# Turning normalized tokens on VectorE in three more groups of a two-layer block, and bias loads on other DMA queues

## The chip, the cores and the metric

The kernel runs on one core of one Trainium2 chip. The metric is device time in microseconds (us), a median of several executions. The engines are TensorE (PE in the profile; PEld is its weight load), VectorE (DVE), ScalarE (ACT), GpSimd (POOL) and SyncE (SP). Each works through its own instructions in the order in which the program issued them, and they wait for one another by semaphores.

## The reference

Two layers work on an image batch of 2 x 56 x 56 positions with 384 channels, 6272 tokens in all, in float32.

Layer 0 is neighbourhood attention (12 heads of 32 channels, a 7 x 7 window that is shifted inwards at the border, a relative position bias) and a two-layer perceptron:

```
h = attention(layer_norm(x));  x = x + h @ w_proj + b_proj
y = layer_norm(x);             x = x + gelu(y @ w1 + b1) @ w2 + b2        # hidden 1536
```

Layer 1 projects to 768 channels, applies a depthwise 3 x 3 convolution, runs an exponential average along rows and columns in both directions, and ends with another perceptron:

```
p = layer_norm(x) @ w_in + b_in
local = depthwise_conv3x3(p)
mixed = 0.25 * (left_right + right_left + top_bottom + bottom_top)(local) + local
x = x + layer_norm(mixed) @ w_out + b_out
x = x + gelu(layer_norm(x) @ w1 + b1) @ w2 + b2
```

## The kernel before

**Three stages.** From 0 to about 700 us the attention of layer 0 runs in windows of 8 x 14 queries. There are 14 groups (two images, seven bands of 8 rows), four windows to a group, three steps to a window (one for each set of four heads), so 12 steps k in group n. Then comes the *first pass* (from about 700 to 1700 us, function `passes`, lines 1418 to 1490): it computes the perceptron of layer 0 and the input projection of layer 1 in 13 groups g of up to four tiles of 128 tokens (sizes 2, 3, 4, 4, ...). The *last pass* (lines 1512 to 1555) computes the output projection of layer 1 and its perceptron, in 13 groups with the sizes reversed.

**Beside the passes** VectorE works on the convolution and the averages. The class `Beside` holds a list of jobs, each a generator of steps. `beside.go(worth)`, called after each piece of matrix work, adds 0.9 (later 1.0) times `worth` to an account and issues steps until their estimated costs have used it up. This settles the order of VectorE's instructions when the program is built. Jobs are added at the end of `project_in` when enough rows of the image are there: the first at the end of group 3 of the first pass. `beside.busy()` says whether jobs are left. The last of them are finished before group 6 of the last pass takes its input (`half_way` is 6).

**Turning tokens into channels.** A layer norm works on tokens (a token on each partition), and the next matrix product needs channels on partitions. There are two ways:

- `channels` calls `to_channels` (line 251): TensorE multiplies each 128 x 128 block with the identity into PSUM (tag `pt`, three banks), 12 such turnings for four tiles of 384 channels, and ScalarE takes the result to SBUF with the norm's gain and shift (line 254).
- `turned` (line 1074) turns one tile on VectorE, SBUF to SBUF, in 16 instructions that each turn three 32 x 32 blocks. `scaled` (line 1081) then applies gain and shift on ScalarE, in place, in three instructions, one for each chunk of 128 channels.

In the first pass `by_vector` chooses: it is true where no convolution is under way, that is in groups 1, 2 and 3. In the last pass it is true from group 6 on.

**The order within a group of the first pass.** Twelve hidden columns (m = 0 to 11) each take three matmuls into one of three banks (`hidden`, line 1090) and one Gelu on ScalarE (line 1099). In their midst stands work on the group before (`waiting`: its tokens have gone through the perceptron of layer 0) and on the next group:

- m=1: `norm_w.shift` on VectorE (line 233), for the group before; m=2 to 5: its tiles are normalized by ScalarE (line 240);
- m=3 to 6, with `by_vector`: `turned` of these tiles on VectorE, one a column, issued ahead of the column;
- m=3: statistics of the next group's tiles on VectorE (line 214); m=5: their shift (line 233); m=7 to 10: ScalarE normalizes them;
- m=6: the group before is stored, after an addition of a row to it (line 1026, on VectorE while there are jobs);
- m=11: `scaled` or `channels` of the group before, ahead of the last column.

Then `project_in` (six columns with `w_in`, line 1090) reads that turned tile `hT_w`; then the next group's tokens are turned for the next hidden columns, and the second matrix of the perceptron is applied tile by tile (`tokens`, line 1106, 24 matmuls a tile, two banks in turn); VectorE adds the residual (line 1478) and takes statistics.

**The order within a group of the last pass.** Twelve hidden columns with the statistics of the next group beside them; `project_out` of the next group (line 1343 takes it); then `tokens` for k = 0 to 3 of this group, with the next group's turning in their midst: at k=1 and k=2 two tiles each on VectorE and `scaled` at k=3, or `channels` at k=3.

**The bias loads.** Attention adds a bias tile for each of three column places, in one buffer each, loaded anew when the band place or image changes: 18 loads, of 1344 KB or 2016 KB (line 317). The first three are issued on SP, the others on ACT's queue. The input x of a group (672 KB, line 302), the values of a window (line 466) and all stores (line 643) go by SP.

Of the kernel before, what the change touches and what calls it, by code (L numbers as in the profile page):

```python
# [40 lines left out]
B, H, W, C = 2, 56, 56, 384  # L41
NH, KS, HD = 12, 7, 32
P = 128
NC = C // P
INNER, NI = 2 * C, 2 * C // P
HID, NHID = 4 * C, 4 * C // P
# [10 lines left out]
NWC = W // QC  # L57
# [29 lines left out]
def place(i, n):  # L87

    return 0 if i == 0 else 2 if i == n - 1 else 1
# [84 lines left out]
def block_kernel(ctx: ExitStack, tc: tile.TileContext, ins: dict, out: bass.AP):  # L174
    nc = tc.nc
# [128 lines left out]
    def spans(place, n, e):  # L304
        return n if place == 1 else e

    def load_bias(n, j):

        b, g = groups_a[n]
        pr, pc = place(g, NG), place(j, NWC)  # L310
        if (b, pr, pc) in biases:
            return
        _, at, size = BIAS_T_AT[pr, pc]
        most = NH * TT * (3 if pc == 1 else 2)
        t = kp.tile([P, most], F32, name=f"bias{pc}")
        queue = nc.sync if n == 0 else nc.scalar
        queue.dma_start(out=t[:, :size], in_=ins["bias_t"][:, at : at + size])
        biases[b, pr, pc] = t[:, :size].rearrange("p (n c q) -> p n c q", n=NH, q=TT)

# [4 lines left out]
    for i in (1, 2, 0):  # L324
        nc.sync.dma_start(out=wqkv[:, :, i * C : (i + 1) * C], in_=w_src[:, :, i * C : (i + 1) * C])
    load_x(1)
    load_bias(0, 0)
    load_bias(0, 1)
    wproj = lp.tile([P, NC, C], F32, name="wproj")
    nc.sync.dma_start(out=wproj, in_=ins["L0_conv_w_proj"].rearrange("(c p) n -> p c n", p=P))  # L330
    shift = lp.tile([P, C], F32, name="shift")
    b_proj = ins["rows"][ROWS["b_proj"] : ROWS["b_proj"] + 1, :]
    nc.sync.dma_start(out=shift, in_=b_proj.to_broadcast([P, C]))
    bq = lp.tile([P, NC], F32, name="bq")


# [268 lines left out]
    groups, dgroups = grouped(sizes), grouped(sizes[::-1])  # L605
# [60 lines left out]
        measure_x(1, k)  # L666
    for m in range(NC, 2 * NC):
        query_or_key(0, m, any_bank)()
    for k in range(NT):
        normalize_x(1, k)  # L670
    for t in tiles_of(0):
# [39 lines left out]
    END, THEN = ng - 2, (7, 9, 11, 13, 16, 19, 22)  # L711
    for s in range(NU + 4):
        n, k, hg, i = s // UG, s % UG, s % NC, s // NC
# [30 lines left out]
        if k == 2 and n + 4 < ng:  # L744
            load_x(n + 4)
        if k == 1 and n < ng:
            load_bias(n, NWC - 1)
        if n + 1 < ng and k in (4, 10):
            load_bias(n + 1, 0 if k == 4 else 1)
        if s == NU - UG - 4:  # L750
            ectx.close()
            wm = ctx.enter_context(tc.tile_pool(name="w_mlp", bufs=1, side="right"))
# [23 lines left out]
        new, before, last = units.get(s), units.get(s - 1), units.pop(s - 2, None)  # L776
# [204 lines left out]
    def passes(xs, xn, w1, w2, between=lambda ps: None):  # L981
# [10 lines left out]
        last = len(groups) - 1  # L992
        half_way = next(g for g, (t, n) in enumerate(dgroups) if t + n * P > T1)
# [417 lines left out]
        for g, (t0, n) in enumerate(groups):  # L1411
            hid = []

            by_vector = 0 < g < last and not beside.busy()
            preparing = prepare_w_out() if g == 1 else iter(())
            if g == last:
                beside.until((0, NI - 1))
                load_row(0, "b2_1")
                ahead = load_mix(0)
            for m in range(NHID):  # L1420
                next(preparing, None)
                if waiting is not None:
                    gw, x2w, norm_w = waiting
                    if m == 1:
                        norm_w.shift(groups[gw][1])
                    if m == 2:
                        xn_w = xp.tile([P, NT, C], F32, name="xn")
                    if 2 <= m < 2 + groups[gw][1]:
                        norm_w.apply_by_scalar(m - 2, x2w, xn_w)
                    if by_vector and m == 2:  # L1430
                        hT_w = io.tile([P, NC, MT], F32, name="hT")
                    if by_vector and 3 <= m < 3 + groups[gw][1]:
                        turned(xn_w, m - 3, hT_w)
                    if m == (11 if g == 1 else 6):
                        store_x2(gw, x2w)
                    if m == NHID - 1 and by_vector:
                        scaled(hT_w, groups[gw][1], *n1)
                    elif m == NHID - 1:
                        hT_w = channels(xn_w, groups[gw][1], *n1)
                hid.append(hidden(w1, m, hT, n, "L0_conv_b1"))  # L1440
                if g < last:
                    if m == 3:
                        x_next, n_next = xs.pop(g + 1), groups[g + 1][1]
                        norm_next = norm_of(x_next, n_next, sm)
                        norm_next.close(n_next)
                    if m == 5:
                        norm_next.shift(n_next)
                    if m == 7:
                        xn_next = xp.tile([P, NT, C], F32, name="xn")
                    if 7 <= m < 7 + n_next:  # L1450
                        norm_next.apply_by_scalar(m - 7, x_next, xn_next)
                    if m == NHID - 1:
                        add_row(x_next, n_next, "b2_0")
                if g == last:
                    measure_beside(m, 0, ahead)
                beside.go(MLP)
            for _ in preparing:
                pass
            if g == 0:
                between(bank())  # L1460
            if waiting is not None:
                project_in(gw, hT_w)
            if g == last:
                w1, w2_1, w_parts = weights(1)
                for part in w_parts[:3]:
                    part()
            if by_vector:
                hT = io.tile([P, NC, MT], F32, name="hT")
                for k in range(n_next):
                    turned(xn_next, k, hT)  # L1470
                scaled(hT, n_next, *ln2)
            elif g < last:
                hT = channels(xn_next, n_next, *ln2)
            x2 = io.tile([P, NT, C], F32, name="xc")
            norm = Norm(sm)
            for k in range(n):
                ps = tokens(hid, w2, k)
                nc.vector.tensor_tensor(x2[:, k, :], ps, x[:, k, :], ALU.add)
                norm.add(k, [x2[:, k, :]])
                if g < last or k < n - 1:  # L1480
                    beside.go(ROW)
            norm.close(n)
            waiting = g, x2, norm
            if g + 2 <= last:
                xs[g + 2] = load_group(x1f, groups[g + 2], "xa")
            if g < last:
                x = x_next
# [4 lines left out]
        g, x2, norm_w = waiting  # L1492
# [17 lines left out]
        n2 = "L1_conv_n2_g", "L1_conv_n2_b"  # L1510
        hT = channels(first["xn"], dgroups[0][1], *n2)
        for g, (t0, n) in enumerate(dgroups):
            by_vector = half_way <= g < last
            hid = []
            for m in range(NHID):
                hid.append(hidden(w1, m, hT, n, "L1_conv_b1"))
                if g < last:
                    measure_beside(m, g + 1, ahead)
                beside.go(MLP_D)
            res = x3  # L1520
            if g < last:
                x3, norm = project_out(g + 1, *ahead)
            if g + 2 <= last and g + 2 != half_way:
                ahead = load_mix(g + 2)
            for k in range(n):
                if by_vector and 0 < k < n - 1:
                    for q in range(2 * k - 2, min(2 * k, dgroups[g + 1][1])):
                        turned(xn, q, hT)
                elif by_vector and k == n - 1:
                    scaled(hT, dgroups[g + 1][1], *n2)  # L1530
                elif k == n - 1 and g < last:
                    hT = channels(xn, dgroups[g + 1][1], *n2)
                ps = tokens(hid, w2, k)
                o = res[:, k, :]
                if k == 0 and g < last:
                    norm.shift(dgroups[g + 1][1])
                if k == 0 and by_vector:
                    xn = normalized(norm, x3, dgroups[g + 1][1])
                    hT = io.tile([P, NC, MT], F32, name="hT")
                if g == last and k == n - 1:  # L1540

                    assert ps is y_end and t0 + n * P == T2
                    nc.vector.tensor_copy(rows[:, 1, :], o)
                    break
                nc.vector.tensor_tensor(o, ps, o, ALU.add)
                nc.sync.dma_start(out=yout[t0 + k * P : t0 + (k + 1) * P, :], in_=o)
                if k == n - 3 and g < last:
                    if not by_vector:
                        xn = normalized(norm, x3, dgroups[g + 1][1])
                    add_row(x3, dgroups[g + 1][1], "b2_1")  # L1550
                beside.go(ROW_D)
            if g + 2 == half_way:
                ahead = load_mix(g + 2)
# [92 lines left out]
```

## Time and profile before

| what | us |
|---|---|
| median of 3 runs | 2662.26 (2661.57 to 2664.49) |
| the profiled execution's own time | 2662.15 |
| its span, first to last instruction | 2660.4 |
| TensorE busy | 2636.8 |
| VectorE busy | 1963.3 |
| ScalarE busy | 898.8 |
| GpSimd busy | 250.2 |
| VectorE, turning tokens (line 1074), 672 instructions of 269 ns | 181.0 |
| TensorE, turning tokens (line 251), 315 of them | 39.0 |
| VectorE, convolution taps (line 1184), 336 instructions | 377.1 |

A line of the timeline gives the start, the length, the engine, the line of the program, the operation, what it writes and reads, its shape and how many instructions are drawn together; in square brackets stands how long the engine was idle before it and what released it. Matmuls overlap each other, so the time between two starts is the price of what lies between them, and not the sum of the lengths. A line of the busy times by stage gives the stretch, its length, the busy time of each engine with its instructions, the granted clock of TensorE (1.00 is full speed), the share of the DMA engines that was busy, and GB/s.

### The profile page before, as it was taken

What the parts mean: (1) busy time and instruction counts of PE and PEld (TensorE: products, weight loads), DVE (VectorE), ACT (ScalarE), POOL (GpSimd) and SP (SyncE); (2) the same over time, 40 slices, a digit from 0 to 9 for tenths busy, and PEclk for the clock granted to TensorE, in tenths of its full rate; (3) what the DMA queues carried; (4) which work ended last, traced back from release to release, by engine and by line L of the source; (5) the groups of instructions that cost most, each with busy time, mean ns of one, the idle gap of its engine ahead of it and who ended that gap; (6) DMA issues with size and microseconds to landing.
All of it is one profiled execution on the core that took longest, in us unless ns stands there. A gap on an engine that the chain in (4) does not pass through costs nothing. (4 is left out here: it accounts for less than half of the span.)

```text
span 2660.4 us, 37315 instructions
## 1 busy us (share of the span) xinstructions
PE 2636.8 (99%) x14987; PEld 1472.0 (55%) x14987; DVE 1963.3 (74%) x3539; ACT 898.8 (34%) x1447; POOL 250.2 (9%) x264
## 2 busy tenths in 40 slices
PE   8999999999999999999999999999999999999999
PEld 5666656666655455555555555555555555555556
DVE  3878877876465698688998889889988737677652
ACT  4655555554322332223344422312134211111111
POOL 0111111110211100000010000000000011100100
PEclk9999999999999999999999999999999999999999
DMA  6422354224410132233346544433355410111000
GB/s 197 155 90 92 130 191 161 73 84 157 161 43 32 65 110 87 86 132 106 121 152 241 185 139 156 178 126 109 103 207 194 180 42 24 45 45 39 30 13 17
DMA packets 131927, 298.98 MB, mean 112 GB/s; under 512 B 10678, under 2 KB 87584, under 8 KB 129440
## 3 DMA queue, kind: packets, MB, share of 16 engines
q1 hardware_dynamic: 126800, 269.76, 29.4%
q10 hardware_dynamic: 4944, 26.74, 2.9%
q8 instruction: 119, 1.95, 0.3%
q14 instruction: 64, 0.52, 0.1%
HBM read 180.86 MB, written 115.61 MB: 111 GB/s over the span
## 5 line engine op out<-in xcount | busy, mean ns | idle before, releaser
L1090 PE MATMUL mm<-hT,w 128*128 128x512 f32 (+2 forms) x1872 | 769.4, 568 | 0.4 <-ACT hT L254 0.2
L1090 PEld LDWEIGHTS mm<-hT,w 128*128 128x128 f32 x1872 | 352.0, 190 | 383.0 <-issue 351.4
L1099 ACT ACTIVATE hid<-mm,chan 128x512 f32<-128x512 f32 (+2 forms) x312 | 206.1, 661 | 671.6 <-PE mm L1090 671.6
L1106 PE MATMUL y_end<-w,hid 128*128 128x384 f32 x1200 | 395.2, 486 | 0.0
L1184 DVE SCALAR_TENSOR_TENSOR loc<-pt,taps,loc 128x990 f32<-128x990 f32 (+9 forms) x336 | 377.1, 1122 | 10.0 <-ACT loc L1166 1.7
L1106 PE MATMUL y<-w,hid 128*128 128x384 f32 x1152 | 379.4, 486 | 0.0
L1106 PEld LDWEIGHTS y_end<-w,hid 128*128 128x128 f32 x1200 | 227.5, 190 | 157.2
L1106 PEld LDWEIGHTS y<-w,hid 128*128 128x128 f32 x1152 | 218.2, 190 | 150.5 <-issue 1.0
L531 DVE TENSOR_TENSOR pts<-sc,bias 119x448 f32<-119x448 f32 (+3 forms) x336 | 221.0, 700 | 72.1 <-PE sc L516 70.0
L537 ACT ACTIVATE pts<-pts 119x448 f32<-119x448 f32 (+3 forms) x336 | 206.6, 642 | 183.3 <-DVE pts L531 183.2
L222 POOL TENSOR_TENSOR rs<-rs,mhalf 128x4 f32<-128x4 f32 (+4 forms) x67 | 87.1, 1300 | 1729.0 <-DVE rs L219 1693.4
L387 PE MATMUL ps<-hT,wqkv 128*128 128x448 f32 x504 | 213.1, 561 | 5.3 <-ACT vs L432 3.2
L1074 DVE STREAM_TRANSPOSE hT<-xn 32x96 f32<-32x96 f32 x672 | 181.0, 269 | 31.3 <-PE mm L1090 11.7
L1090 PE MATMUL mm<-hT,w_in 128*128 128x512 f32 (+2 forms) x468 | 191.9, 568 | 0.6 <-ACT hT L254 0.6
L240 ACT ACTIVATE xn<-xc,sh,rs 128x384 f32<-128x384 f32 x98 | 64.7, 698 | 269.3 <-DVE sh L233 269.2
L1090 PEld LDWEIGHTS mm<-hT,w_in 128*128 128x128 f32 x468 | 88.5, 190 | 102.1 <-issue 90.6
L387 PEld LDWEIGHTS ps<-hT,wqkv 128*128 128x128 f32 x504 | 90.6, 192 | 86.8 <-issue 73.2
L516 PEld LDWEIGHTS sc<-qT,kT 32*100 32x100 f32 (+3 forms) x3168 | 90.7, 169 | 66.4 <-issue 16.0
L1316 DVE STREAM_TRANSPOSE turned<-mx 32x192 f32<-32x192 f32 x336 | 123.3, 367 | 4.2
L516 PE MATMUL sc<-qT,kT 32*100 32x112 f32 (+3 forms) x3168 | 113.4, 270 | 5.9 <-DVE pts L531 4.7
L557 PE MATMUL o<-pts,vt 100*32 100x112 f32 (+3 forms) x3168 | 111.2, 264 | 1.5 <-ACT og L479 1.0
L425 PE MATMUL ps<-wqkv,hT 128*128 128x384 f32 x294 | 106.9, 502 | 0.0
(106 smaller groups left out, 2645.1 us busy)
## 6 DMA issues: line engine op xcount, KB each, us to landing
loc<-loc_d SPq DMA_DIRECT2D x24, 784.0 KB
mixed<-mix_d SPq DMA_DIRECT2D x24, 784.0 KB
mix_d<-mixed SPq DMA_DIRECT2D x24, 784.0 KB
bias<-in_bias_t ACTq DMA_DIRECT2D x13, 1344.0 KB
xa<-x_d SPq DMA_DIRECT2D x22, 768.0 KB
p_d<-mx SPq DMA_DIRECT2D x10, 1536.0 KB
mx<-mix_d SPq DMA_DIRECT2D x10, 1536.0 KB
pt<-p_d SPq DMA_DIRECT2D x18, 560.0 KB
```

The lines of the kernel that those rows point to most:

```text
L387: nc.tensor.matmul(ps, lhsT=wqkv[:, c, m * P : (m + 1) * P], rhs=hT[:, c, half_of(n)], start=c == 0, stop=c == NC - 1,)
L425: nc.tensor.matmul(ps, lhsT=hT[:, c, at : at + P], rhs=wqkv[:, c, 2 * C :], start=c == 0, stop=c == NC - 1,)
L516: nc.tensor.matmul(sc[i // 2][: w.keys, i % 2, (first + c) * TT : (first + c + 1) * TT], lhsT=kT[d, hg, w.keys_at + r * w.kc : w.keys_at + ...
L531: nc.vector.tensor_tensor(self.of(half), sc[half][:n, :, at].rearrange("p h (c q) -> p h c q", q=TT), self.w.bias[:n, 4 * self.hg + h : 4 ...
L537: nc.scalar.activation(self.of(half), self.of(half), AF.Exp)
L557: nc.tensor.matmul(o[i * HD : (i + 1) * HD, hg, :], lhsT=w.vt[:n, c, h * HD : (h + 1) * HD], rhs=self.pts[:n, i, c, :], start=c == 0, stop ...
L1074: nc.vector.transpose(hT[j : j + HD, :, k * P + i : k * P + i + HD], xn[i : i + HD, k, :].rearrange("p (c q) -> p c q", c=NC)[:, :, j : j ...
L1090: nc.tensor.matmul(ps[:, : n * P], lhsT=w[:, c, m * P : (m + 1) * P], rhs=hT[:, c, : n * P], start=c == 0, stop=c == NC - 1,)
L1099: nc.scalar.activation(t[:, : n * P], ps[:, : n * P], AF.Gelu, bias=col(b1, m))
L1106: nc.tensor.matmul(ps, lhsT=t[:, k * P : (k + 1) * P], rhs=w[:, m, :], start=m == 0, stop=m == len(lhs) - 1,)
L1184: nc.vector.scalar_tensor_tensor(to, pt[:, lo + dy - self.top : hi + dy - self.top, xt : xt + n], self.tap(dy, dx), to, ALU.mult, ALU.add,)
L1316: nc.vector.transpose(t[j : j + HD].rearrange("p (m c) -> p m c", m=NI)[:, :, i : i + HD], mx[i : i + HD, :, k * P + j : k * P + j + HD],)
```

## The change

The first-pass groups 4 and 5, which have convolution beside them, turn the tokens of the group before by VectorE (`n1_by_vector`) in place of TensorE; the next group's tokens are still turned by TensorE there. The last pass turns by VectorE one group sooner: in group 5 for the tokens of group 6. The first two bias loads, the attention's output weights and a row are issued on ACT's queue after the first group's keys were computed, in place of SP's queue at the very start. The later bias loads are issued on SP, but for those of the last attention group, which stay on ACT.

```diff
--- before.py
+++ after.py
@@ -304,7 +304,7 @@
     def spans(place, n, e):
         return n if place == 1 else e
 
-    def load_bias(n, j):
+    def load_bias(n, j, queue=nc.sync):
 
         b, g = groups_a[n]
         pr, pc = place(g, NG), place(j, NWC)
@@ -313,7 +313,6 @@
         _, at, size = BIAS_T_AT[pr, pc]
         most = NH * TT * (3 if pc == 1 else 2)
         t = kp.tile([P, most], F32, name=f"bias{pc}")
-        queue = nc.sync if n == 0 else nc.scalar
         queue.dma_start(out=t[:, :size], in_=ins["bias_t"][:, at : at + size])
         biases[b, pr, pc] = t[:, :size].rearrange("p (n c q) -> p n c q", n=NH, q=TT)
 
@@ -324,13 +323,9 @@
     for i in (1, 2, 0):
         nc.sync.dma_start(out=wqkv[:, :, i * C : (i + 1) * C], in_=w_src[:, :, i * C : (i + 1) * C])
     load_x(1)
-    load_bias(0, 0)
-    load_bias(0, 1)
     wproj = lp.tile([P, NC, C], F32, name="wproj")
-    nc.sync.dma_start(out=wproj, in_=ins["L0_conv_w_proj"].rearrange("(c p) n -> p c n", p=P))
     shift = lp.tile([P, C], F32, name="shift")
     b_proj = ins["rows"][ROWS["b_proj"] : ROWS["b_proj"] + 1, :]
-    nc.sync.dma_start(out=shift, in_=b_proj.to_broadcast([P, C]))
     bq = lp.tile([P, NC], F32, name="bq")
 
 
@@ -666,6 +661,11 @@
         measure_x(1, k)
     for m in range(NC, 2 * NC):
         query_or_key(0, m, any_bank)()
+
+    load_bias(0, 0, nc.scalar)
+    nc.scalar.dma_start(out=wproj, in_=ins["L0_conv_w_proj"].rearrange("(c p) n -> p c n", p=P))
+    nc.scalar.dma_start(out=shift, in_=b_proj.to_broadcast([P, C]))
+    load_bias(0, 1, nc.scalar)
     for k in range(NT):
         normalize_x(1, k)
     for t in tiles_of(0):
@@ -744,9 +744,9 @@
         if k == 2 and n + 4 < ng:
             load_x(n + 4)
         if k == 1 and n < ng:
-            load_bias(n, NWC - 1)
+            load_bias(n, NWC - 1, nc.scalar if n > END else nc.sync)
         if n + 1 < ng and k in (4, 10):
-            load_bias(n + 1, 0 if k == 4 else 1)
+            load_bias(n + 1, 0 if k == 4 else 1, nc.scalar if n >= END else nc.sync)
         if s == NU - UG - 4:
             ectx.close()
             wm = ctx.enter_context(tc.tile_pool(name="w_mlp", bufs=1, side="right"))
@@ -1412,6 +1412,7 @@
             hid = []
 
             by_vector = 0 < g < last and not beside.busy()
+            n1_by_vector = by_vector or g in (4, 5)
             preparing = prepare_w_out() if g == 1 else iter(())
             if g == last:
                 beside.until((0, NI - 1))
@@ -1427,13 +1428,13 @@
                         xn_w = xp.tile([P, NT, C], F32, name="xn")
                     if 2 <= m < 2 + groups[gw][1]:
                         norm_w.apply_by_scalar(m - 2, x2w, xn_w)
-                    if by_vector and m == 2:
+                    if n1_by_vector and m == 2:
                         hT_w = io.tile([P, NC, MT], F32, name="hT")
-                    if by_vector and 3 <= m < 3 + groups[gw][1]:
+                    if n1_by_vector and 3 <= m < 3 + groups[gw][1]:
                         turned(xn_w, m - 3, hT_w)
                     if m == (11 if g == 1 else 6):
                         store_x2(gw, x2w)
-                    if m == NHID - 1 and by_vector:
+                    if m == NHID - 1 and n1_by_vector:
                         scaled(hT_w, groups[gw][1], *n1)
                     elif m == NHID - 1:
                         hT_w = channels(xn_w, groups[gw][1], *n1)
@@ -1510,7 +1511,7 @@
         n2 = "L1_conv_n2_g", "L1_conv_n2_b"
         hT = channels(first["xn"], dgroups[0][1], *n2)
         for g, (t0, n) in enumerate(dgroups):
-            by_vector = half_way <= g < last
+            by_vector = half_way - 1 <= g < last
             hid = []
             for m in range(NHID):
                 hid.append(hidden(w1, m, hT, n, "L1_conv_b1"))
```

## The prediction

> **What bounds the kernel now.** I read the page first, then the busy time by stage, then the timelines of TensorE, VectorE and ScalarE in the groups that the change touches.
>
> ```profile
> span 2660.4 us, 37315 instructions
> PE 2636.8 (99%) x14987; PEld 1472.0 (55%) x14987; DVE 1963.3 (74%) x3539; ACT 898.8 (34%) x1447; POOL 250.2 (9%) x264
> ```
>
> TensorE is busy for 99% of the span; its idle time is 2660.4 - 2636.8 = 23.6 us in all. So the end is set by TensorE's work plus its stalls, and a change can gain only what it takes off TensorE or out of these 23.6 us, but can lose much by a new wait in front of TensorE. By stage (columns: TensorE, weight loads, VectorE, ScalarE, GpSimd busy, clock, DMA share, GB/s):
>
> ```profile
> 868.00:945.00 77.00, 77.00 (x204) 38.57 (x203) 52.39 (x160) 22.53 (x33) 8.88 (x4) 1.00 0.16 56
> 945.00:1025.00 80.00, 80.00 (x230) 41.33 (x229) 67.81 (x68) 25.32 (x36) 3.92 (x2) 1.00 0.34 123
> 1025.00:1105.00 80.00, 80.00 (x230) 41.35 (x229) 52.60 (x57) 23.02 (x34) 4.95 (x2) 1.00 0.23 81
> ...
> 2107.00:2189.00 82.00, 82.00 (x255) 45.12 (x254) 25.32 (x42) 12.87 (x19) 12.28 (x5) 1.00 0.25 87
> ```
>
> These are first-pass groups 3, 4 and 5 and last-pass group 5. Over a whole group, VectorE seems to have room: 12.2 us in group 4, 27.4 us in group 5, 56.7 us in the last. What counts is where the room lies. TensorE in group 4:
>
> ```profile
> 945.02 28.49 PE L1090 MATMUL mm<-hT,w 128*128 128x512 f32 x66
> 973.34 1.47 PE L251 MATMUL tp<-ident,xn 128*128 128x128 f32 x12
> 974.65 2.74 PE L1090 MATMUL mm<-hT,w 128*128 128x512 f32 x6
> 977.23 15.61 PE L1090 MATMUL mm<-hT,w_in 128*128 128x512 f32 x36
> ```
>
> Eleven of twelve hidden columns, the 12 turnings that go, the last column, and at 977.23 the input projection, which reads what was turned. VectorE in the same group:
>
> ```profile
> 957.66 0.55 DVE L214 BATCH_NORM_STATS2 st<-xa 128x6 f32<-128x384 f32 x1
> ...
> 960.53 5.35 DVE L1184 SCALAR_TENSOR_TENSOR loc<-pt,taps,loc 128x1045 f32<-128x1045 f32 x4
> 965.79 0.15 DVE L233 SCALAR_TENSOR_TENSOR sh<-mv,rs 128x4 f32<-128x4 f32 x1
> ...
> 967.14 1.75 DVE L1026 TENSOR_TENSOR xc<-xc,rows 128x1536 f32<-128x1536 f32 x1
> ```
>
> 957.66 is the statistics of column m=3, 965.79 the shift of m=5, 967.14 the row addition of m=6. VectorE has no idle time between 945.35 and here but 0.91 us for GpSimd's power; its first real rest (5.97 us) comes at 995.96. So its room lies after the projection has begun. Last, group 3, where the same tokens are turned by VectorE already, without convolution:
>
> ```profile
> 874.43 4.51 DVE L1074 STREAM_TRANSPOSE hT<-xn 32x96 f32<-32x96 f32 x16 [3.60 <-ACT xn L240]
> ...
> 881.85 9.03 DVE L1074 STREAM_TRANSPOSE hT<-xn 32x96 f32<-32x96 f32 x32
> ...
> 890.99 4.50 DVE L1074 STREAM_TRANSPOSE hT<-xn 32x96 f32<-32x96 f32 x16
> ```
>
> A tile costs 4.51 us, and the last ends at 895.49; the projection starts at 898.61. Without one convolution step in between, the margin is 3.1 us less the scaling on ScalarE.
>
> [...] 16 instructions of 269 ns for a tile of 384 channels on VectorE. [...] TensorE stands from 25.53 to 27.02 after two broken microseconds, and the granted clock is 0.50 from 27 to 33. [...] the trace shows 0.33 us of issue for a bias load on ACT[...].
>
> **The change, part by part.**
>
> 1. *TensorE's turnings go (gain).* First-pass groups 4 and 5 and last-pass group 5 lose 12 turnings each. Price: 974.65 - 973.34 = 1.31 us a set (group 4 lasts 79.93 us against group 3's 77.31, two sets more: 2.62). 3 x 1.31 = 3.9 us off TensorE. The three evictions (2.10 us on ScalarE) become three scalings of 2.22 us: nothing.
>
> 2. *VectorE turns in group 4 (loss).* 64 instructions, 4 x 4.51 = 18.0 us, put ahead of the steps of m=3 to 6. VectorE works in order, and tokens are ready before it (normalizing ends from 954.8 on), so they push the later instructions by their whole length. The fourth tile stands just ahead of the 967.14 row: it ends at 967.14 + 18.04 = 985.2. ScalarE's scaling of the first chunk takes 0.74 us with some 0.2 us of signalling: TensorE can begin at 986.1, and the second and third chunks follow at 0.74 us each where a matmul needs 0.43: 0.6 more. It would have begun at 977.23 - 1.31 = 975.9. Net against before: 986.1 + 0.6 - 977.23 = +9.5 us, with the gain of its 1.31 in it. The same delay arrives in two pieces: the shift of m=5 comes three tiles later, at 979.3, so ScalarE, which at m=7 normalizes the next group with it, holds up the activations of columns 8 to 11; with three banks for columns TensorE stops at 973.35 until about 980.8. The last column then fits into the wait for the fourth tile, so this isn't added twice.
>
> 3. *VectorE turns in group 5.* Convolution runs out at 1065.7, too late as well: the row addition of m=6 is at 1048.18, the fourth tile ends at 1066.2, TensorE begins at 1067.1, plus 0.6, against 1057.16: +10.6 us. Group 4's delay doesn't shorten this: VectorE is level with TensorE again at the end of group 4 (18.0 us more work against 12.2 idle and 9.5 of later end), as its row additions follow TensorE.
>
> 4. *Clock.* The stop of 7.5 us should halve it. The last column at half clock takes 5.15 instead of 2.58 us and ends at about 986.0, just as the tokens come; what is left is under 1 us each time. I take 0.3 each, +0.6; bounds 0 and 3 each (the start's slow stretch lasted 6 us, half of it lost).
>
> 5. *Last-pass group 5.* VectorE works 25.3 of 82 us; group 6 does the same beside more work (59.1 of 80) without a stall. Its 18.0 us lie under 31 us of token matmuls: -1.31 us, already priced; without this cover it would be like 2.
>
> 6. *Start.* Bias (2 x 1344 KB), wproj and shift leave SP, where they stood behind x of group 1, for ACT behind the key copies (about 17.8). Group 1's x landed at 17.35; without traffic beside it I estimate 14 to 15 from 3.1 MB at the 250 to 318 GB/s of the stages. But ACT now issues four DMAs (0.33 each as in the later rows, to 1.0 as on SP here) ahead of its normalizing, and the loads now run when the first value stores leave (24.51 before, landed in 2 us), which hold the third value copy, for which TensorE waits 1.49 us. Gain at most 2.3 us of gaps from 22 to 27 plus 3.0 of slow clock; loss up to 3 us by later stores. I take 0; ends -5 and +3.
>
> 7. *Later bias loads move from ACT to SP* (12 of 15; those of the last group stay). ACT saves 0.33 us each, where it is half idle: 0. On SP they stand ahead of value loads, residual loads and x1 stores, for which SP waits. In the trace such a store after a bias load already took 6 us to land[...]; 1344 KB in front of it takes about as long. Value loads are three steps of 3.8 us early. I take 0; ends -2 (the 1.25 us stall at 321.00 and its like) and +4.
>
> Sum: the profiled execution's own time is 2662.15 (span 2660.4 and 1.75 around it), 0.11 below the median 2662.26. +9.5 +10.6 +0.6 -1.3 = +19.4, so 2681.6 beside the median.
>
> **Rivals.** *A, the start gains:* -5.3, so 2676.3. For: x of group 1 is what VectorE waits 8.65 us for. Against: the value stores. *B, the clock stays low into the projection:* 2.7 more each, 2687. For: 6 us after the start's gap. *C, SP's queue holds up value stores and so ScalarE:* +4, 2685.6[...]. *D, faster: VectorE's turning is covered.* It decides at one point: whether the fourth tile ends by 975.0 in group 4 and 1054.9 in group 5. Then the price is -3.9, with the start 0 to -5: 2653 to 2658. For: 12 to 27 us of room in each group. Against: VectorE would have to be 10 us earlier, and its order of instructions is fixed. That the edit does nothing can't be: group 4 and 5 carry turnings on TensorE in the trace.
>
> **How the numbers follow.** Forecast 0.58, own range 2677 to 2686; A 0.14, B 0.10, C 0.06, D 0.12 (0.07 faster by over 0.2%, about what a measurement of this kernel can tell from no change; 0.05 within it, if the start loses). So faster 0.07, same 0.05, slower 0.88. The range from 2673 to 2689 takes in A, B and C with their bounds and leaves out D.
>
> **What would show it.** Right: TensorE idle before the w_in columns of groups 4 and 5, some 7 us at the twelfth hidden column and 1 to 2 at the projection, ended by ScalarE, which waits for VectorE's shift and turning; group 4 lasts about 89 us, group 5 about 90.5; clock under 1 there; last-pass group 5 at 80.0 us instead of 81.3. Wrong: no such gap (D), or a start, from 0 to 60 us, with a TensorE busy time more than 3 us from 53.6 (A).

## The result and the profile after

The changed kernel takes 2683.43 us (median of 4 runs, 2681.28 to 2683.70) against 2663.38 us for the kernel before, measured beside it (4 runs): a ratio of 1.0074, 95% interval 1.0061 to 1.0086. The forecast was 2681.6. The profiled execution took 2681.28 us with a span of 2679.5, 19.1 us longer than the 2660.4 of before.

The page after, its span and busy times:

```profile
span 2679.5 us, 37444 instructions
PE 2636.2 (98%) x14951; PEld 1469.4 (55%) x14951; DVE 2013.7 (75%) x3731; ACT 898.6 (34%) x1447; POOL 250.6 (9%) x264
```

TensorE has 36 matmuls fewer, yet its idle time rose from 23.6 to 43.3 us. Its busy time fell by only 0.6 us, because matmuls are busy for longer where the granted clock is 0.50 (at the end of group 4, from 982.50 to 985.91, two start 0.85 us apart in place of 0.43). VectorE has 192 instructions and 50.4 us more. Who TensorE waited for, over the whole execution (columns: microseconds in all, times, longest):

```profile
PE mm L1090 <- ACT hid L1099: 14.6, 2, 7.4
PE ps L382 <- ACT vs L427: 7.5, 1, 7.5
PE sc L511 <- DVE pts L526: 5.2, 8, 1.3
PE mm L1090 <- ACT hT L1081: 2.4, 2, 1.8
```

The first and the fourth line are new, two each: the twelfth column and the projection of first-pass groups 4 and 5. The second was 3.2 us in three pieces before: the 1.5 us of the start have become 7.5, and the two in attention are gone. The third was 4.7.

TensorE in group 4, the answer to the four lines shown of before (eleven columns, then the last, then the projection):

```profile
946.61 28.49 PE L1090 MATMUL mm<-hT,w 128*128 128x512 f32 x66
982.47 4.54 PE L1090 MATMUL mm<-hT,w 128*128 128x512 f32 x6 [7.37 <-ACT hid L1099]
987.59 15.72 PE L1090 MATMUL mm<-hT,w_in 128*128 128x512 f32 x36 [0.59 <-ACT hT L1081]
```

Two stops, 7.37 and 0.59 us, and between them a column that takes 4.54 us in place of 2.74. VectorE in the same group:

```profile
959.25 4.50 DVE L1074 STREAM_TRANSPOSE hT<-xn 32x96 f32<-32x96 f32 x16
963.79 0.56 DVE L214 BATCH_NORM_STATS2 st<-xa 128x6 f32<-128x384 f32 x1
...
969.22 4.51 DVE L1074 STREAM_TRANSPOSE hT<-xn 32x96 f32<-32x96 f32 x16
973.76 2.67 DVE L1184 SCALAR_TENSOR_TENSOR loc<-pt,taps,loc 128x1045 f32<-128x1045 f32 x2
976.35 4.50 DVE L1074 STREAM_TRANSPOSE hT<-xn 32x96 f32<-32x96 f32 x16
980.88 0.16 DVE L233 SCALAR_TENSOR_TENSOR sh<-mv,rs 128x4 f32<-128x4 f32 x1
980.96 1.30 DVE L1184 SCALAR_TENSOR_TENSOR loc<-pt,taps,loc 128x1045 f32<-128x1045 f32 x1
982.18 4.51 DVE L1074 STREAM_TRANSPOSE hT<-xn 32x96 f32<-32x96 f32 x16
986.72 1.76 DVE L1026 TENSOR_TENSOR xc<-xc,rows 128x1536 f32<-128x1536 f32 x1
```

The four tiles stand one a column, with statistics and convolution taps between them and no idle time. The shift, which the next group's normalizing needs, comes after the third tile. ScalarE shows what that does:

```profile
981.13 0.71 ACT L240 ACTIVATE xn<-xa,sh,rs 128x384 f32<-128x384 f32 x1 [12.98 <-DVE sh L233]
981.75 0.67 ACT L1099 ACTIVATE hid<-mm,chan 128x512 f32<-128x512 f32 x1
...
986.73 2.22 ACT L1081 ACTIVATE hT<-hT,chan 128x512 f32<-128x512 f32 x3 [0.30 <-DVE hT L1074]
```

ScalarE stands 12.98 us in front of one normalizing, with the Gelu of a column behind it, and so holds the bank that the twelfth column needs.

By stage (group 4, group 5, last-pass group 5):

```profile
946.60:1035.40 88.80, 80.84 (x217) 40.50 (x216) 84.63 (x132) 25.31 (x36) 3.92 (x2) 0.96 0.31 111
1035.40:1125.40 90.00, 80.96 (x218) 40.54 (x217) 69.66 (x121) 22.89 (x34) 4.95 (x2) 0.96 0.20 72
2125.00:2207.00 82.00, 82.00 (x248) 44.70 (x247) 45.21 (x107) 12.97 (x19) 12.28 (x5) 1.00 0.25 87
```

Group 4 lasts 88.81 us (79.93 before), group 5 89.94 (79.94 before), last-pass group 5 79.97 (81.29 before), each from one first hidden column to the next; every other group is within 0.04 us of before. The first hidden column of all starts at 703.32 (701.73 before). 8.88 + 10.00 - 1.32 + 1.59 = 19.15, the whole difference.

The start shows a third stop. TensorE after, at the queries of the first group:

```profile
31.23 9.88 PE L382 MATMUL ps<-hT,wqkv 128*128 128x448 f32 x18 [7.46 <-ACT vs L427]
```

It was 27.02 with a stop of 1.49. ScalarE's third copy of values waits 7.6 us for a store; SP's issues of the three stores, after and then before (the length of such a row takes in SP's wait between two of its stores):

```profile
22.76 8.77 SPq L638 DMA_DIRECT2D v_d<-vs  x3
```

```profile
24.51 2.80 SPq L643 DMA_DIRECT2D v_d<-vs  x3
```

The issuing itself is short. After the change, all stores to `v_d` up to 60 us (least, median and longest in ns), and the third of the three:

```profile
L638 SPq DMA_DIRECT2D v_d<-vs x5: 320/345/477, 22.8 to 45.6; - x5
```

```profile
31.20 0.32 SPq L638 DMA_DIRECT2D v_d<-vs  x1
```

Two stores leave at once; the third can't leave before the third copy is made, and that copy waits for the first store to land.

### The profile page after: what moved, and what is told of

Its sections match the earlier page's. It is cut to its first block, busy times and chain, and to the rows that moved or that the text cites. A ratio compares the mean times of both kernels' runs of the same rounds, so it can differ in the third digit from the quotient of the medians.

```text
span 2679.5 us, 37444 instructions
## 1 busy us (share of the span) xinstructions
PE 2636.2 (98%) x14951; PEld 1469.4 (55%) x14951; DVE 2013.7 (75%) x3731; ACT 898.6 (34%) x1447; POOL 250.6 (9%) x264
## 5 line engine op out<-in xcount | busy, mean ns | idle before, releaser
L1074 DVE STREAM_TRANSPOSE hT<-xn 32x96 f32<-32x96 f32 x864 | 232.7, 269 | 33.9 <-PE mm L1090 11.8
```

Source lines behind the costliest of these rows:

```text
L1074: nc.vector.transpose(hT[j : j + HD, :, k * P + i : k * P + i + HD], xn[i : i + HD, k, :].rearrange("p (c q) -> p c q", c=NC)[:, :, j : j ...
```

## The experiments

Each kernel was timed beside the kernel before on one chip in five rounds. The theory: the price is the place of the turning in VectorE's order, ahead of what TensorE waits for, in groups 4 and 5; the other parts come to a few microseconds. Rivals: the moved DMAs carry the loss; VectorE has too much work wherever it stands.

| run | ratio to before (95%) | span of the profiled execution |
|---|---|---|
| queues alone | 1.0011 (1.0003 to 1.0019) | 2663.9 |
| turning in 4 and 5 alone | 1.0068 (1.0054 to 1.0082) | 2678.3 |
| last-pass group 5 alone | 0.9990 (0.9982 to 0.9998) | 2662.2 |
| change, three value buffers | 1.0043 (1.0029 to 1.0056) | 2676.3 |
| turning, convolution held | 1.0073 (1.0059 to 1.0087) | 2679.1 |
| queues, loads later | 0.9996 (0.9988 to 1.0004) | 2658.2 |
| turning, shift first | 1.0088 (1.0074 to 1.0102) | 2682.8 |
| change, three buffers, held | 1.0049 (1.0035 to 1.0063) | 2672.2 |
| three buffers, no turning in 4 and 5 | 0.9973 (0.9963 to 0.9983) | 2655.5 |
| before, three value buffers | 0.9978 (0.9971 to 0.9985) | 2655.8 |
| change, three buffers, held, rate 1.05 | 1.0071 (1.0057 to 1.0085) | 2676.4 |
| turning, held, rate 1.05 | 1.0110 (1.0095 to 1.0126) | 2679.8 |

### The three parts, each alone

*Queues alone*, of the change:

```diff
-            n1_by_vector = by_vector or g in (4, 5)
+            n1_by_vector = by_vector
-            by_vector = half_way - 1 <= g < last
+            by_vector = half_way <= g < last
```

> The change's DMA queues alone, with the turning as before. Theory (the price of the change is the turning in groups 4 and 5; the queues cost 4.2 us at the start and give back 1.4, 0.5 and 0.7 us in attention): 1.6 us slower than before, granted clock at half for some 6 us after a stop of 7.5 us before 31 us. Rival (the queues carry a larger part of the 19 us, for instance by transfers that are late in the passes): more than 5 us slower.

*Turning in groups 4 and 5 alone*: the kernel before with `n1_by_vector` as in the change and the last pass as before.

> The turning by VectorE in first-pass groups 4 and 5 alone, with the queues and the last pass as before. Theory (the turning stands in VectorE's order ahead of what TensorE waits for): 18.9 us slower than before, group 4 lasts 88.8 us in place of 79.9, group 5 89.9 in place of 79.9. Rival (the stops come only together with the other queues, which delay the convolution's transfers): under 5 us slower.

*Last-pass group 5 alone*: the kernel before with `half_way - 1`.

> The turning by VectorE in last-pass group 5 alone. Theory (covered by idle time of VectorE): 1.3 us faster than before, that group 80.0 us in place of 81.3. Rival (the scaling comes too late for the next hidden columns): same or slower.

Measured: +2.9 us for the queues (2662.55 x 0.0011), +18 us for the turning, -2.7 us for the last pass (interval -4.8 to -0.5); 18.3 in sum, within the intervals of the 20 of the change. By stage, the turning alone gives groups of 88.78 and 89.92 us, the last pass alone 79.96 us. With the queues alone no group of either pass differs from before by more than 0.02 us; TensorE stops 7.62 us at the start. So the turning carries the loss by itself, and the rival that the queues carry it falls. The two small parts can't be read from the spans: three of the executions that share one program up to 700 us begin the passes at 701.73 (before), 700.80 (turning) and 704.93 (last pass). By estimate their difference is mostly half clock at other places (the section on hardware below), so for parts of this size I go by the stages.

### The start

*Three value buffers* in the changed kernel (in `shift_by_values`, which shares the buffers, likewise):

```diff
-            vs = ep.tile([P, C], F32, name="vs", bufs=2)
+            vs = ep.tile([P, C], F32, name="vs", bufs=3)
```

> The changed kernel with a third buffer for the values' copies (vs). Theory (at the start the third value copy waits until the first value store has landed behind the bias loads; that stops TensorE for 7.5 us and halves its clock): 10 us faster than the changed kernel, so 9 us slower than before, no stop before 31 us and the clock full throughout the first 60 us. Rival (TensorE waits at the start for the loads themselves): the same as the changed kernel, 19 us slower than before.

*Loads later*: the queues alone, with the four loads on ACT behind the value copies.

```diff
-    load_bias(0, 0, nc.scalar)
-    nc.scalar.dma_start(out=wproj, in_=ins["L0_conv_w_proj"].rearrange("(c p) n -> p c n", p=P))
-    nc.scalar.dma_start(out=shift, in_=b_proj.to_broadcast([P, C]))
-    load_bias(0, 1, nc.scalar)
...
     for t in tiles_of(0):
         store_all()
         value(t, any_bank)()
+    load_bias(0, 0, nc.scalar)
+    nc.scalar.dma_start(out=wproj, in_=ins["L0_conv_w_proj"].rearrange("(c p) n -> p c n", p=P))
+    nc.scalar.dma_start(out=shift, in_=b_proj.to_broadcast([P, C]))
+    load_bias(0, 1, nc.scalar)
```

> As the queues alone, but the four loads on ACT stand behind the first group's three value copies instead of behind its key copies. Theory (the loads hold up the first value store, whose landing the third copy waits for): the store lands 2 us after its issue, TensorE stops 1.5 us before the queries instead of 7.6, about 25.3 instead of 31.5, so 6 us faster than the queues alone, some 3 us faster than before. Rival (the loads are needed later and are now late): a new stop between 45 and 60 us, same as the queues alone.

With three buffers the changed kernel takes 2675.62, some 8 us less than itself, where 10 were expected. Its TensorE at the start:

```profile
22.59 1.68 PE L353 MATMUL ps<-ident,xg 112*128 112x112 f32 x12
24.10 6.96 PE L382 MATMUL ps<-hT,wqkv 128*128 128x448 f32 x18
```

No stop between turning and queries, which begin at 24.10 in place of 31.23 and take 6.96 us in place of 9.88. The stop was the third copy's wait for a free buffer, that is for the first store to land, and not for the loads themselves; the rival falls. With the loads later the queries begin at 25.18 after a stop of 1.45, about the 1.49 of before, so by estimate the store lands in about 2 us again. That version is 2661.74, 4.0 us less than the queues alone, where 6 were expected, and as fast as before within its interval. Its trace shows where 2 us went: the input of group 2 now lands behind the loads (VectorE takes it at 37.43 in place of 32.31), and TensorE's twelve turnings of it last from 43.08 to 46.27, with short waits, where they took 1.2 us before. So the rival (the loads come late) holds in a small way. The place of the loads accounts for the long stop, and what else the moved loads bring is too small for these runs.

*The kernel before with three buffers*, nothing else, and *the change with three buffers without turning in groups 4 and 5*:

> The kernel before with a third buffer for the value copies, nothing else. Theory (the stops for a value copy at the start, at 321 and at 412 us are all the wait for a buffer): these three stops (1.5, 1.3 and 0.4 us) go, and the start's half clock goes or becomes shorter: 3 to 6 us faster than before. Rival (what the change's queues gain in attention needs the queues): only the start's stop goes, 1.5 us faster.

> The changed kernel with a third buffer for the value copies and without the turning in groups 4 and 5: its queues and its last-pass group 5. Theory: start 4.8 us, attention 1.8 us and last pass 1.3 us earlier than before: about 8 us faster, 2654. Rival (the half-clock windows late in attention take the start's gain back): 3 us faster.

Both beat both kernels: 2656.32 and 2655.57 against 2662.93, and they are the same within their intervals. In the first, the stops at 321 and 412 us are gone as well, so the one buffer does what the moved bias loads did there. The queues add nothing to it that these runs can tell.

### Is it VectorE's order or its load?

*Shift first*: the turning alone, with the next group's statistics and shift ahead of the tiles.

```diff
-                    if m == 3:
+                    if m == (1 if n1_by_vector and not by_vector else 3):
-                    if m == 5:
+                    if m == (2 if n1_by_vector and not by_vector else 5):
```

> As the turning in groups 4 and 5 alone, but there the next group's statistics are taken at m=1 and its shift at m=2, ahead of the turning. Theory (the stop at the twelfth column is the shift behind three tiles, the stop at the projection is the fourth tile, and both are one delay of VectorE): the stop at the twelfth column goes, a single stop of about 9 us stands before the projection, and the group is not shorter; it may be up to 3 us longer, since the half clock now falls into the projection. Rival (two separate costs): groups 4 and 5 some 7 us shorter each.

TensorE in group 4:

```profile
943.43 31.06 PE L1090 MATMUL mm<-hT,w 128*128 128x512 f32 x72
984.31 15.89 PE L1090 MATMUL mm<-hT,w_in 128*128 128x512 f32 x30 [9.81 <-ACT hT L1081]
```

All twelve columns run through, and one stop of 9.81 us stands before the projection; in group 5 it is 11.04. The groups last 91.45 and 92.43 us, 2.7 and 2.5 longer than with the shift behind. The two stops are one delay, and in two pieces it is cheaper, since the column at half clock (4.54 us, clock 0.50 from 979.08 to 985.91 in the change) then lies inside it; here the projection runs while the clock is 0.71 on average (984 to 994).

*Convolution held* in columns 0 to 6 of groups 4 and 5, on the turning alone:

```diff
-                beside.go(MLP)
+                if by_vector or not n1_by_vector or m >= 7:
+                    beside.go(MLP)
```

> As the turning in groups 4 and 5 alone, but columns 0 to 6 of these two groups give the convolution nothing, so its steps come later, in group 5's idle time. Theory (the price is the place in VectorE's order: some 10 us of convolution steps stand ahead of the fourth tile): both stops go, groups 4 and 5 last 78.6 us each, 2.6 us faster than before and 21 us faster than with the turning alone. Rival (VectorE's 18 us a group are too many wherever they stand): stops move to the token matmuls or to the projection, groups 4 and 5 together still more than 5 us over the 159.9 of before.

TensorE in group 4, and in last-pass group 5:

```profile
942.96 31.06 PE L1090 MATMUL mm<-hT,w 128*128 128x512 f32 x72
974.59 15.72 PE L1090 MATMUL mm<-hT,w_in 128*128 128x512 f32 x36 [0.56 <-ACT hT L1081]
```

```profile
2128.98 0.71 PE L1305 MATMUL xi<-ident,mx 128*128 128x128 f32 x5
2140.42 0.45 PE L1305 MATMUL xi<-ident,mx 128*128 128x128 f32 x1 [10.73 <-DMA mx<-mix_d]
```

The stops are down to 0.56 and 0.72 us, and the groups last 79.45 and 79.61: their price was what stood ahead of the tiles in VectorE's order. But the time is as bad as with the turning alone. What was held comes due later: from first-pass group 12 to the second group of the last pass 4.2 us more go by, and last-pass groups 3 and 5 are 5.7 and 12.6 us longer. In groups 12 and 5 TensorE waits for mixed inputs that the convolution finishes late, in group 3 for VectorE's statistics (2.84 us). With 2.1 us less up to the passes and 1.7 less in groups 4, 5 and 10 the execution is 18.7 us longer than before.

*The change with three buffers and the same hold:*

> The changed kernel with a third buffer for the value copies and with no convolution steps in columns 0 to 6 of groups 4 and 5. Theory: start 4.8 us and attention 1.8 us earlier than before, groups 4 and 5 shorter by 2.6 us together, last-pass group 5 by 1.3: 10 us faster than before, about 2652. Rival (the freed time is taken up by other waits): not faster than before by more than 5 us.

It comes to 2675.63, as the three buffers without the hold: the same stops at the mixed inputs (10.68 us the longest). The expected gain failed.

*Paying the debt back*: both held kernels with the convolution's account filled faster.

```diff
+            if g == 5:
+                beside.rate = 1.05
...
-                beside.rate = 1.0
+                beside.rate = 1.05
```

> As the turning in groups 4 and 5 alone with the convolution held in columns 0 to 6, and the rate of 1.05 from group 5 on. Theory: no stops at the mixed inputs; groups 4 and 5 together 0.8 us shorter than before and nothing else changed: 1 us faster than before. Rival: the debt of some 17 us stays as stops anywhere, 15 us or more slower than before.

> As the changed kernel with three value buffers and without convolution steps in columns 0 to 6 of groups 4 and 5, but the convolution's account is filled at a rate of 1.05 from group 5 on (0.9 and 1.0 before). Theory (what the held steps left undone came back as stops at the mixed inputs of last-pass groups 0 and 6): these stops go, groups 4 and 5 stay at 79.5 us each, about 9 us faster than before, 2653. Rival (VectorE has no more time in groups 6 to 12): the stops stay, or new ones stand at the token matmuls, still slower than before.

Both go to the rivals. The 10.7 us stop is gone, but first-pass groups 6 to 10 last 80.2 to 83.8 us in place of 79.9 to 80.8, 12.0 us in sum with three buffers, and stops of 3.6 and 3.9 us stay where the last pass takes its inputs. TensorE's waits in the kernel with three buffers, 1060 to 1990 us:

```profile
PE mm L1090 <- ACT hT L254: 7.2, 3, 3.6
PE xi L1305 <- DVE st L214: 3.9, 1, 3.9
PE mm L1090 <- ACT hid L1099: 3.6, 2, 2.7
PE xi L1305 <- DMA mx<-mix_d: 3.6, 1, 3.6
```

The stage after group 5, of this kernel and then of the kernel before:

```profile
1103.00:1183.00 80.00, 77.28 (x223) 39.95 (x222) 77.39 (x78) 25.46 (x36) 4.71 (x2) 1.00 0.35 120
```

```profile
1103.00:1183.00 80.00, 80.00 (x230) 41.35 (x229) 69.29 (x71) 25.15 (x36) 3.74 (x2) 1.00 0.34 120
```

VectorE is busy 77.4 of 80 us there, comes late with a shift, ScalarE waits for it, and TensorE for ScalarE: the same chain as in group 4, one group on. The timed runs of the kernel with two buffers spread wider (2681.6 to 2693.0, median 2689.3) than those of any other, and the profiled execution is the fastest of them. The three slower ones have a mean granted clock of 0.995 where it has 0.998; by estimate that is 0.003 x 2690 = 8 us, most of the difference. Why their clock was lower isn't known.

## Why the prediction was right, step by step

The direction, the place and the mechanism in groups 4 and 5 are right. That the size came out so close is in part luck: the two groups were put 1.8 us too high (20.7 with the clock, measured 18.88) and the attention before them 1.6 us too low (0, measured +1.59).

1. *Turnings off TensorE*: right. Last-pass group 5 shows it bare: 1.32 us for a forecast 1.31.
2. *Group 4*: forecast +9.5 and +0.3 for the clock, measured +8.88. The two pieces came as worked out: stop of 7.37 for 7.5 at the twelfth column, end of the fourth tile 40.1 us after the group's start for 40.2. The last column took 4.54 us at half clock for the 5.15 assumed. The 0.6 us for the second and third chunk didn't appear (the projection's 36 records took 15.72 us for 15.61). That term was a misreading: the 0.43 us belongs to one of the profile's records, and these matmuls have two each. That is why eleven columns of three matmuls are x66, and also why a tile of tokens shows 24 where the program issues twelve. So TensorE works 0.86 us on a chunk, longer than ScalarE's 0.74 for the next. The clock had no part in it: it was full again at 985.91, and the projection began at 987.59. *Shift first* shows that the stops must not be added.
3. *Group 5*: forecast +10.6 and +0.3, measured +10.00, with stops of 7.21 and 1.83; too high by the same two terms.
4. *Clock*: half for 6.8 us in each group (979.08 to 985.91 and 1067.84 to 1074.67), as the step had it. That a stop would halve it was an estimate; the trace of before has one low stretch (26.15 to 32.97), at the start. The last column ended before the fourth tile was ready, so of the 0.3 us each nothing was left. Rival B (low clock into the projection) fell with it in these two groups; *Shift first* shows what it costs: 2.7 and 2.5 us a group, where B had 2.7.
5. *Last pass*: right, covered as argued.
6. *Start*: the step failed in size. It took 0, with 3 us as its worst end; measured +4.2 us at the queries. Its mechanism was named (value stores behind the loads), but its price rested on stores that come "up to 3 us" later. The store took 7.9 us from issue to the copy that waits for it, against 2.0. TensorE was busy for 48.9 of the first 60 us in place of 53.6, so the prediction's own sign for rival A (more than 3 us from 53.6) came true, but by a loss and not by A's gain. The x of group 1 did land earlier (VectorE takes it at 15.59 in place of 17.35), and the turning then ran without a break; the later stop swallowed that.
7. *Later bias loads*: it took 0, with -2 as its best end; measured about -1.9 from two stops: 1.4 us less at 321, 0.5 at 412. In the queues alone and in the kernel before with three buffers the same two stops are gone. Both were ScalarE's wait for a value store, 3.5 us at 321 before and 1.2 after. So rival C had the sign wrong. Before: a bias load, the store of attention's output behind it, the load that SP issues once that store has landed, and the first value store:

```profile
298.55 0.33 ACTq L317 DMA_DIRECT2D bias<-in_bias_t  x1
299.54 0.33 SPq L643 DMA_DIRECT2D x_d<-xr  x1
305.56 0.34 SPq L572 DMA_DIRECT2D xr<-in_x  x1
...
317.76 0.37 SPq L643 DMA_DIRECT2D v_d<-vs  x1
```

After, where TensorE is 4.2 us later at this place:

```profile
297.33 0.34 SPq L316 DMA_DIRECT2D bias<-in_bias_t  x1
303.64 0.33 SPq L638 DMA_DIRECT2D x_d<-xr  x1
306.35 0.33 SPq L567 DMA_DIRECT2D xr<-in_x  x1
...
317.92 0.38 SPq L638 DMA_DIRECT2D v_d<-vs  x1
```

On SP the load leaves at 297.33, just after VectorE's last read of the old tile (it ends at 296.19 + 1.12 = 297.31); on ACT it left at 298.55, 5.35 us after that read (292.08 + 1.12 = 293.20), behind work that ACT began at 297.84. It is 6.3 us ahead of the output's store in place of 1.0, that store lands after 2.7 us in place of 6.0, and SP comes to the value store 3.4 us after the copy (it ends at 314.48) in place of 7.4. That the one follows from the other is read from these times; no run tests it alone.

Together 6 and 7 and a stop of 0.43 us at 697.72 that is gone after (0.6 us; TensorE waited for VectorE's residual) came to +1.6 us by the start of the passes. In these two executions no half clock falls between 40 us and the passes. The forecast's 0 was near by offsetting errors.

Rival D (turning is covered) fell at its own point: the fourth tile of group 4 ended 40.1 us after the group's start, 10 us later than that point. *Convolution held* shows that the point was the right one: with that tile on time the groups are 0.4 us shorter than before. What the forecast didn't see is that the two reorderings tried here, held steps with and without a faster account, don't keep this gain, since what moves away comes back later as a debt. A finer spreading of the convolution, or fewer tiles turned by VectorE, wasn't tried.

## What to carry to other kernels

An engine's idle share over a stage doesn't say that work fits in: look at where in its order the idle time stands, and add what you insert to the position of the instruction that the bound engine waits for. Work that runs "beside" has a due time of its own; moving it out of the way only pays if the engine has room before that due time. In a timeline, a row's length is not the cost of its instructions where the engine waits between them. A wait for a buffer to be stored is cheap to find (the copy's releaser is a DMA) and one more buffer was worth some 6 us here, more than the change could have gained at its best estimate of 3.9 us off TensorE.

## What the runs showed of the hardware

*Half clock came in stretches of 6.8 and 10.2 us, and differed between executions of one program.* In the change the granted clock is 0.50 from 26.76 to 37.00, from 979.08 to 985.91 and from 1067.84 to 1074.67, in the kernel before from 26.15 to 32.97; in the rest of both traces it is 1.00 up to the last microsecond. The busy times of the change, group 4:

```profile
975.67:979.08 3.41, 0.00 (x0) 0.00 (x0) 3.29 (x11) 0.00 (x0) 0.00 (x0) 1.00 0.01 2
979.08:985.91 6.83, 3.44 (x4) 1.51 (x5) 6.54 (x23) 4.78 (x8) 0.00 (x0) 0.50 0.01 2
985.91:989.32 3.41, 2.82 (x7) 1.05 (x6) 3.35 (x5) 3.11 (x5) 0.00 (x0) 1.00 0.00 0
```

TensorE did nothing in the 3.41 us ahead of this fall, and nothing from 1064.43 to 1067.84 ahead of the one in group 5. Ahead of the rise it had worked since 982.47, for 3.44 us. The length wasn't set by the stop alone: stops of 7.37 and 7.21 us came with 6.8 us in groups 4 and 5, but the stop of 7.46 us at the start of the change came with 10.2. In *Shift first* the mean clocks of 0.83 (971 to 984) and 0.71 (984 to 994) come to some 10.2 us at half clock beside the stop of 9.81 us, by estimate (2 x 0.17 x 13 + 2 x 0.29 x 10).

At the start, after stops of 1.49, 1.50 and 1.47 us, the first queries took 9.97 us in the kernel before, and 7.03 us both in the turning with the convolution held and in the same with the rate of 1.05, whose program is that of before up to the passes. Late in attention, at 651.58, six matmuls (`ps<-wproj,og`) took 2.97 us in the three-buffer kernel with the rate of 1.05, and 2.20 at the same place of the change (659.33); by estimate half clock fell there, too. Over the whole execution the last pass alone has a mean granted clock of 0.998, where before has 0.999; by estimate that is 0.001 x 2660 = 2.7 us, most of the 3.2 us by which its passes begin after those of before (704.93 and 701.73).

The prediction puts the low clock of the start of before at 27 to 33 us. It begins sooner, and TensorE wasn't idle for the 3.41 us ahead of it:

```profile
22.74:26.15 3.41, 1.94 (x11) 1.20 (x11) 0.00 (x0) 2.12 (x5) 0.00 (x0) 1.00 0.51 179
26.15:32.97 6.82, 5.95 (x8) 2.86 (x9) 0.63 (x2) 2.98 (x5) 0.00 (x0) 0.50 0.79 223
```

In these 3.41 us TensorE was busy for 1.94 us, with turnings, and the stop of 1.49 us, from 25.53 on, had only begun. What made the clock fall there no run here shows.

*A small store beside large loads of another queue.* The first of the value stores, 192 KB, landed after some 7.9 us (issued at 22.76, the copy that waits for it starts at 30.70) in place of 2.0 (24.51 and 26.49 before). ACT had issued 3456 KB of loads from 16.80 to 18.78 us; from 22.76 to 30.70 its queue still moved 1.79 MB, and SP's queue 0.39 MB. With these loads issued later TensorE's stop was 1.45 us in place of the 7.62 of the queues alone. How the loads hold the store up no run here shows.
